# Moving one exchanged copy to ScalarE and loading four pieces together in a convolution chain with a recurrent first layer

## The chip, the cores and the metric

The kernel runs on one core of one Trainium2 chip. The metric is the device time of one execution in microseconds (us). The core has five engines with queues of their own: PE (TensorE, matmuls; its weight loads are listed as PEld), DVE (VectorE), ACT (ScalarE), POOL (GpSimd) and SP (SyncE, which here starts most of the DMA transfers). An engine works through its own instructions; between engines, order is kept by semaphores.

## The reference

Four layers follow each other on a batch of 16 images with 32 channels of 128 x 128, each with a normalisation ahead of it or a residual behind it. Two places matter here.

The first layer is a diagonal LSTM. The image is skewed, so that step t sees the diagonal column t, and 128 steps follow each other; each needs the hidden state of the step before, at its own row and at the row above:

```python
def step(carry, xt):
    pc, ph = carry
    ph_shift = jnp.pad(ph, ((0, 0), (0, 0), (1, 0)))[:, :, :-1]
    s2s = jnp.einsum('oc,bch->boh', W1_prev, ph_shift) + jnp.einsum('oc,bch->boh', W1_cur, ph) + b1[None, :, None]
    g = xt + s2s
    o = jax.nn.sigmoid(g[:, 0 * bo:1 * bo])
    f = jax.nn.sigmoid(g[:, 1 * bo:2 * bo])
    i = jax.nn.sigmoid(g[:, 2 * bo:3 * bo])
    gg = jnp.tanh(g[:, 3 * bo:4 * bo])
    nc = f * pc + i * gg
    nh = o * jnp.tanh(nc)
    return ((nc, nh), nh)
```

At step t only the rows up to t differ from each other: every later row has seen no input yet, and all such rows carry the same state. So a kernel needs to compute t + 1 rows and one more that stands for the rest.

The second layer quantises its input to 8 bits and takes sums of absolute differences with the weights:

```python
qx = _ste_quant(x, INPUT_SCALE)       # shift, clamp to +-127, round
...
return -jnp.sum(jnp.abs(pr - wk[None, :, None]), axis=1)   # for each output channel
```

The third layer (a Hartley transform) and the fourth (a small U-Net) are not touched by the change.

## The kernel before

The recurrent stage works in 16 chunks of T = 8 steps. The batch is split into two chains (c = 0, 1), each with two groups of images, so that one chain can compute while the other waits. In a chunk, n = min(8(ch + 1) + 2, 128) rows are computed. `rows(ch)` gives this n; when a new chunk begins, the rows that come in are set from the last row of the chunk before (line 210):

```python
for ch in range(NT):
    n = rows(ch)
    following = load(ch + 1) if ch + 1 < NT else None
    if ch:
        m = rows(ch - 1)
        for c in range(2):
            for v in (hs[c][(ch - 1) % 2][:, T - 1, :, 1:], ex[c][0][:, :, 1:], cs[c]):
                if n > m:
                    nc.vector.tensor_copy(v[:, :, m:n], bcast(v[:, :, m - 1], 2, n - m))   # L210
    for j in range(T):
        t = T * ch + j
        for c in range(2):
            h_in = (hs[c][ch % 2][:, j - 1] if j else hs[c][(ch - 1) % 2][:, T - 1], ex[c][t % 2])
            ...
            # 24 products into PSUM tile pg: 8 each with xn, with h and with e (L223)
            ...
            for q in (F, I, G, O):
                nc.scalar.activation(gt[:, q, :, :n], place[q][:, :, :n],          # L243
                                     AF.Tanh if q == G else AF.Sigmoid, bias=...)
            nc.vector.tensor_mul(cell, cell, gt[:, F, :, :n])                      # L250
            nc.vector.tensor_mul(ig[:, :, :n], gt[:, I, :, :n], gt[:, G, :, :n])   # L251
            nc.vector.tensor_add(cell, cell, ig[:, :, :n])                         # L252
            nc.scalar.activation(th[:, :, :n], cell, AF.Tanh)                      # L254
            nc.vector.tensor_mul(h_out[:, :, 1 : n + 1], gt[:, O, :, :n], th[:, :, :n])   # L255
            for half in range(2):
                own, other = slice(64 * half, 64 * half + 64), slice(64 - 64 * half, 128 - 64 * half)
                nc.vector.tensor_copy(ex[c][(t + 1) % 2][own, :, 1 : n + 1],
                                      h_out[other, :, 1 : n + 1])                  # L258
        # residual additions and statistics of one group: L185, L188, L189
        # normalisation of the next chunk's input on ScalarE: L174
        ...
```

`e` (the tile `ex`) is h with its two halves of 64 partitions exchanged. A product of 64 x 64 reads its operand from one half of the partitions; with h and e both halves of the PE array have work at once. A tile has 2n elements in each partition, so the shape 128x196 in the profile stands for n = 98 rows.

A scheduler decides in which order the instructions of this stage stand on each engine; within an engine the order is then fixed.

After the stage, the first image is quantised in four pieces before the second layer can begin. The pieces go through the pool `self.xp`, which has two buffers:

```python
def unquantised(self, b, i):
    t = self.xp.tile([128, 8 * W], F32, name="xq")
    self.nc.sync.dma_start(t, jc_rows(self.d["x1"], b, i // 2, 8 * (i % 2), 8))    # L482
    return t
def scaled(self, b, t):
    self.nc.scalar.activation(t, t, AF.Identity, bias=..., scale=...)              # L486
def quantise(self, b, i, t):
    qt = self.ring[i % 2]                       # two tiles in turn
    nc.vector.tensor_scalar(qt[:, :, 1 : W + 1], v, RND, RND, ALU.add, ALU.subtract)   # L493
    nc.vector.tensor_scalar(flat, flat, -127.0, 127.0, ALU.max, ALU.min)               # L495
    self.weave.later(4.0, lambda: nc.sync.dma_start(to, flat))                         # L498
...
for i in range(4):
    t = self.unquantised(0, i)
    self.scaled(0, t)
    self.quantise(0, i, t)
    weave.due(float("inf"))                     # starts the store now
before, following = None, self.loaded(0, 0)     # L505: reads the quantised image back, as tile q
```

`jc_rows` addresses a piece as 4 x 32 runs of 4 KB. Everything after this, up to the end of the kernel, is recorded in a fixed order.

Of the kernel before, what the change touches and what calls it, by code (L numbers as in the profile page):

```python
# [7 lines left out]
F32 = mybir.dt.float32  # L8
# [7 lines left out]
B, C, H, W = 16, 32, 128, 128  # L16
# [32 lines left out]
def bcast(ap, dim, n):  # L49

    dims = [list(x) for x in ap.ap]
    dims.insert(dim, [0, n])
    return bass.AP(ap.tensor, ap.offset, dims)
# [47 lines left out]
def stage0(nc, tc, keep, cst, x, xs, w0, b1, b2, x1):  # L101
# [5 lines left out]
    T = 8  # L107
# [4 lines left out]
    with ExitStack() as ctx:  # L112
# [3 lines left out]
        with tc.tile_pool(name="s0_ld", bufs=4) as ld, tc.tile_pool(name="s0_ps", bufs=2, space=PSUM) as ps:  # L116
            for g in range(NG):
                for q in range(4):
                    t = ld.tile([128, 32 * W], F32, name="x_in")
# [25 lines left out]
        hs = [[sm.tile([128, T, 2, H + 1], F32, name=f"h_{c}_{i}") for i in range(2)] for c in range(2)]  # L145
        ex = [[sm.tile([128, 2, H + 1], F32, name=f"e_{c}_{i}") for i in range(2)] for c in range(2)]
        cs = [sm.tile([128, 2, H], F32, name=f"c_{c}") for c in range(2)]
# [15 lines left out]
        def load(ch):  # L163
            steps = slice(T * ch * H, T * (ch + 1) * H)
            xn = [xp.tile([128, NG, T, H], F32, name=f"xn{i}") for i in range(2)]
            res = rp.tile([128, NG, T, H], F32, name="res")
            for g in range(NG):
                nc.sync.dma_start(flat(xn[0], g), bc_view(xs, g)[:, steps])
                nc.sync.dma_start(flat(res, g), bc_view(x, g)[:, steps])
            return xn, res  # L170

        def normalise(ch, xn, g):
            v = xn[0][:, g, :, : T * (ch + 1)]
            nc.scalar.activation(v, v, AF.Identity, bias=shift[:, g : g + 1], scale=r0[:, g : g + 1])  # L174
            for half in range(2):
                own, other = slice(64 * half, 64 * half + 64), slice(64 - 64 * half, 128 - 64 * half)
                nc.sync.dma_start(flat(xn[1], g)[own], flat(xn[0], g)[other])

        def add(ch, res, g, half):

            n = rows(ch)
            steps = slice(T // 2 * half, T // 2 * (half + 1))
            h = hs[g // 2][ch % 2][:, steps, g % 2]
            r = res[:, g, steps, :n]
            nc.vector.tensor_add(r, r, h[:, :, 1 : n + 1])  # L185
            if n < H:
                r = res[:, g, steps, n:]
                nc.vector.tensor_add(r, r, bcast(h[:, :, n], 2, H - n))  # L188
            nc.vector.bn_stats(stat1[:, g, 2 * ch + half, :], flat(res, g)[:, 512 * half : 512 * half + 512])  # L189
            if half:  # L190
                nc.sync.dma_start(bc_view(x1, g)[:, T * ch * H : T * (ch + 1) * H], flat(res, g))

        def rows(ch):

            return min(T * (ch + 1) + 2, H)
# [4 lines left out]
        with tc.tile_pool(name="s0_gps", bufs=2, space=PSUM) as gps:  # L200
            for ch in range(NT):
                n = rows(ch)
                following = load(ch + 1) if ch + 1 < NT else None
                if ch:

                    m = rows(ch - 1)
                    for c in range(2):
                        for v in (hs[c][(ch - 1) % 2][:, T - 1, :, 1:], ex[c][0][:, :, 1:], cs[c]):
                            if n > m:
                                nc.vector.tensor_copy(v[:, :, m:n], bcast(v[:, :, m - 1], 2, n - m))  # L210
                for j in range(T):
                    t = T * ch + j
                    for c in range(2):
                        h_in = (hs[c][ch % 2][:, j - 1] if j else hs[c][(ch - 1) % 2][:, T - 1], ex[c][t % 2])
                        h_out, cell = hs[c][ch % 2][:, j], cs[c][:, :, :n]
                        pg = gps.tile([128, 2, 2, 2, H], F32, name=f"pg{c}")
                        place = {q: pg[:, i, k] for i, b in enumerate(BANK) for k, q in enumerate(b)}

                        def product(kind, k, i, pair, v, width):

                            q = BANK[i][k]
                            half = slice(64 * (pair ^ i), 64 * (pair ^ i) + 64)
                            nc.tensor.matmul(  # L223
                                place[q][64 * pair : 64 * pair + 64, :, :width],
                                wb[half, 4 * kind + KIND[q]].rearrange("p b o -> p (b o)"),
                                v[half],
                                start=kind == 2 and k == 0,
                                stop=kind == 1,
                                skip_group_check=True,
                            )  # L230

                        for k in range(2):
                            for i in range(2):
                                for pair in range(2):
                                    product(2, k, i, pair, xn[i][:, 2 * c : 2 * c + 2, j, : t + 1], t + 1)
                        for k in range(2):
                            for kind in range(2):
                                for i in range(2):
                                    for pair in range(2):
                                        product(kind, k, i, pair, h_in[i][:, :, 1 - kind : n + 1 - kind], n)  # L240
                        gt = gp.tile([128, 4, 2, H], F32, name=f"gt{c}")
                        for q in (F, I, G, O):
                            nc.scalar.activation(  # L243
                                gt[:, q, :, :n],
                                place[q][:, :, :n],
                                AF.Tanh if q == G else AF.Sigmoid,
                                bias=bias[:, KIND[q] : KIND[q] + 1],
                            )
                        ig = gp.tile([128, 2, H], F32, name=f"ig{c}", bufs=1)
# [3 lines that stand above are left out]
                        th = gp.tile([128, 2, H], F32, name=f"th{c}")  # L253
                        nc.scalar.activation(th[:, :, :n], cell, AF.Tanh)  # L254
                        nc.vector.tensor_mul(h_out[:, :, 1 : n + 1], gt[:, O, :, :n], th[:, :, :n])  # L255
                        for half in range(2):
                            own, other = slice(64 * half, 64 * half + 64), slice(64 - 64 * half, 128 - 64 * half)
                            nc.vector.tensor_copy(ex[c][(t + 1) % 2][own, :, 1 : n + 1], h_out[other, :, 1 : n + 1])  # L258
                    if j >= T // 2:
                        add(ch, res, j - T // 2, 0)  # L260
                        if following:
                            normalise(ch + 1, following[0], j - T // 2)
                    elif ch:
                        add(ch - 1, previous, j, 1)
                previous = res
                if following:
                    xn, res = following
            for g in range(NG):
                add(NT - 1, previous, g, 1)
                nc.vector.bn_aggr(mv[:, g, :], stat1[:, g].rearrange("p a b -> p (a b)"))  # L270
# [16 lines left out]
def jc_rows(t, b, half, at=0, rows=16):  # L287

    first = t.offset + b * CHW + (64 * half + at) * W
    return bass.AP(t.tensor, first, [[16 * W, 4], [HW, C], [1, rows * W]])  # L290
# [123 lines left out]
class Differences:  # L414
# [61 lines left out]
                self.ring[0].rearrange("p r w -> p (r w)")[:, : 4 * P].rearrange("p (a w) -> p a w", w=P),  # L476
            )

    def unquantised(self, b, i):

        t = self.xp.tile([128, 8 * W], F32, name="xq")
        self.nc.sync.dma_start(t, jc_rows(self.d["x1"], b, i // 2, 8 * (i % 2), 8))  # L482
        return t

# [75 lines left out]
    def run(self, tc, ctx, weave):  # L560
        nc, R, P = self.nc, self.R, self.P
# [3 lines left out]
        self.qp = ctx.enter_context(tc.tile_pool(name="s1_q", bufs=2, side="right"))  # L565
        dp = ctx.enter_context(tc.tile_pool(name="s1_d", bufs=2, side="right"))
        ps = ctx.enter_context(tc.tile_pool(name="s1_ps", bufs=4, space=PSUM))
        for i in range(4):
            t = self.unquantised(0, i)
            self.scaled(0, t)  # L570
            self.quantise(0, i, t)
            weave.due(float("inf"))
        before, following = None, self.loaded(0, 0)
        for b in range(B):
            for half in range(2):
                q = following
                late, ahead, xq = [], [], {}
                for i in range(72):
# [26 lines left out]
                    t = dp.tile([128, R, P], F16, name="d_act" if act else "d_dve", bufs=2 if act else 3)  # L605
# [1211 lines left out]
```

## Time and profile before

| | |
|---|---|
| time, median of 3 runs | 7892.06 us (7889.79 to 7894.32) |
| span of the profiled execution | 7884.7 us |
| busy PE, PEld, DVE, ACT | 5635.8, 3165.4, 5847.9, 5406.7 us |
| recurrent stage | about 94 to 838 us of the span |
| first quantisation, until the second layer's first difference | about 838 to 935 us |
| mean granted clock of PE | 0.842 |

A window of the profile gives the busy time of each engine between two moments; the timeline lists instructions in order of time, those that follow each other in one group merged into one row (x4 is four instructions), with the idle time ahead of them in brackets, and after the arrow what ended it. A group of instructions is listed with its shapes and number, then its busy time and the mean of one in ns, then the idle time ahead of it. Waits are put down to whatever came last.

### The profile page before, as it was taken

Reading aid. Unit: us, or ns where it says so; the run is one execution under the profiler, and the core shown is the slowest. Engines: PE = TensorE matmul, PEld = TensorE weight load, DVE = VectorE, ACT = ScalarE, POOL = GpSimd, SP = SyncE. Lnnn points to the kernel's source line nnn. Section 1 sums busy time; section 2 is a strip of 40 time slices with the busy share of each in tenths; the row PEclk is TensorE's granted clock in tenths of the full one; section 3 lists DMA queues with packets and bytes.
Section 4 is the critical chain, followed back from the end, with each engine's and each line's share of the span. In section 5 each row is a group of like instructions: output and inputs, shape, how many; then the busy total and the mean of one; then the engine's idle time right before and its main releaser. Section 6 shows DMA issues by size and latency. Waiting matters only on the chain. (4 is left out here: it accounts for less than half of the span.)

```text
span 7884.7 us, 258419 instructions
## 1 busy us (share of the span) xinstructions
PE 5635.8 (71%) x121132; PEld 3165.4 (40%) x121132; DVE 5847.9 (74%) x7177; ACT 5406.7 (69%) x3129; POOL 21.6 (0%) x15
## 2 busy tenths in 40 slices
PE   3788366566677668886676666897667765997797
PEld 3665222222253334442343343343335333555564
DVE  7787599989969797887877978888787877134213
ACT  2565488799869879887778877887887885123122
POOL 0000000000000000000000000000000000000000
PEclk9899788888878779998868788998787887897896
DMA  8653111111132431112332432120333233434314
GB/s 319 223 181 130 59 50 60 48 52 39 50 116 80 123 102 51 58 33 67 79 98 90 129 89 73 40 70 34 88 86 101 87 102 94 116 107 122 91 33 90
DMA packets 374269, 721.68 MB, mean 92 GB/s; under 512 B 50896, under 2 KB 219856, under 8 KB 362320
## 3 DMA queue, kind: packets, MB, share of 16 engines
q1 hardware_dynamic: 372768, 704.58, 29.4%
q8 instruction: 949, 15.55, 0.8%
q14 instruction: 120, 0.98, 0.0%
q10 hardware_dynamic: 432, 0.57, 0.0%
HBM read 507.21 MB, written 164.32 MB: 85 GB/s over the span
## 5 line engine op out<-in xcount | busy, mean ns | idle before, releaser
L610 ACT ACTIVATE d_act<-q,neg 128x8192 f16<-128x8192 f16 (+1 forms) x612 | 4332.5, 7137 | 930.9 <-PE acc L536 877.6
L614 DVE TENSOR_SCALAR d_dve<-q,qw 128x8192 f16<-128x8192 f16 (+1 forms) x1692 | 3906.2, 2361 | 512.0 <-PE acc L536 476.3
L536 PE MATMUL acc<-d_dve,sel 128*32 128x512 f16 x27072 | 2007.5, 432 | 861.6 <-DVE d_dve L614 838.8
L536 PEld LDWEIGHTS <-sel 128*32 128x32 f16 x36864 | 1121.1, 106 | 2800.6 <-issue 2196.8
L536 PE MATMUL acc<-d_act,sel 128*32 128x512 f16 x9792 | 784.5, 446 | 499.1 <-ACT d_act L610 494.7
L1519 PE MATMUL acc<-xp,wf 32*32 32x512 f32 x25600 | 986.0, 625 | 29.0 <-issue 16.1
L1519 PEld LDWEIGHTS acc<-xp,wf 32*32 32x32 f32 x25600 | 478.8, 105 | 378.1 <-issue 244.6
L1458 ACT ACTIVATE y<-pooled,b 32x128 f32<-32x128 f32 x512 | 204.6, 400 | 532.2 <-DVE pooled L1444 525.1
L223 PE MATMUL pg<-h,wb 64*64 64x20 f32 (+15 forms) x4096 | 401.2, 323 | 102.4 <-DVE h L255 67.0
L753 PE MATMUL acc<-y,u_conv 32*32 32x256 f32 (+1 forms) x9728 | 402.2, 511 | 79.3 <-issue 35.8
L223 PE MATMUL pg<-e,wb 64*64 64x20 f32 (+15 forms) x4096 | 353.2, 318 | 24.7 <-DVE e L258 10.0
L243 ACT ACTIVATE gt<-pg,bias 128x20 f32<-128x20 f32 (+15 forms) x1024 | 302.7, 377 | 84.2 <-PE pg L223 80.0
L1204 PE MATMUL acc<-xp 32*64 32x204 f32 (+3 forms) x8576 | 247.3, 368 | 130.0 <-ACT xp L1170 107.8
L552 PE MATMUL acc<-q,sel 32*32 32x512 f16 x4608 | 158.6, 556 | 204.9 <-DVE xr L519 115.1
L223 PEld LDWEIGHTS pg<-h,wb 64*64 64x64 f32 x4096 | 243.7, 156 | 140.5 <-DVE h L255 97.6
L223 PEld LDWEIGHTS pg<-e,wb 64*64 64x64 f32 x4096 | 250.6, 158 | 108.3 <-DVE e L258 77.9
L223 PE MATMUL pg<-xn,wb 64*64 64x8 f32 (+60 forms) x4096 | 267.9, 304 | 25.3 <-ACT gt L243 17.4
L1616 ACT ACTIVATE xr<-xr,l_ms 128x1024 f32<-128x1024 f32 x64 | 70.4, 1141 | 305.6 <-DVE xr L1611 254.3
L753 PEld LDWEIGHTS acc<-y,u_conv 32*32 32x32 f32 x9728 | 189.7, 119 | 220.0 <-issue 126.5
L1164 ACT ACTIVATE xp<-xp,fr_shift,stats 128x1280 f32<-128x1280 f32 (+1 forms) x128 | 181.7, 1431 | 136.1 <-DMA xp<-x_d 73.9
L1204 PEld LDWEIGHTS acc<-xp 32*64 32x64 f32 (+1 forms) x8576 | 199.3, 147 | 187.8 <-ACT xp L1170 118.0
L254 ACT ACTIVATE th<-c 128x20 f32<-128x20 f32 (+15 forms) x256 | 81.9, 320 | 222.2 <-DVE c L252 221.2
(203 smaller groups left out, 4247.9 us busy)
## 6 DMA issues: line engine op xcount, KB each, us to landing
xr<-x_d SPq DMA_DIRECT2D x192, 512.0 KB
xp<-x_d SPq DMA_DIRECT2D x112, 640.0 KB
q<-q_d SPq DMA_DIRECT2D x32, 2145.0 KB
x_d<-xr SPq DMA_DIRECT2D x128, 512.0 KB
x_in<-in_x_dram SPq DMA_DIRECT2D x16, 2048.0 KB
res<-in_x_dram SPq DMA_DIRECT2D x64, 512.0 KB
xn<-in_xs_dram SPq DMA_DIRECT2D x64, 512.0 KB
xn<-xn SPq DMA_DIRECT2D x128, 256.0 KB
```

Source lines behind the costliest of these rows:

```text
L223: nc.tensor.matmul(place[q][64 * pair : 64 * pair + 64, :, :width], wb[half, 4 * kind + KIND[q]].rearrange("p b o -> p (b o)"), v[half], s ...
L243: nc.scalar.activation(gt[:, q, :, :n], place[q][:, :, :n], AF.Tanh if q == G else AF.Sigmoid, bias=bias[:, KIND[q] : KIND[q] + 1],)
L254: nc.scalar.activation(th[:, :, :n], cell, AF.Tanh)
L536: self.nc.tensor.matmul(acc[k][32 * j : 32 * j + 32, :], self.sel16[:, i // 9, :], d[:, row : row + 4, c : c + W], start=False, stop=i == 71,)
L552: self.nc.tensor.matmul(acc[k][32 * j : 32 * j + 32, :], self.sel16[rows, 8, :], q[rows, row : row + 4, kw : kw + W], start=tap == 0, stop ...
L610: nc.scalar.activation(dst, src, AF.Relu, bias=self.neg[:, i : i + 1])
L614: nc.vector.tensor_scalar(dst, src, self.qw[:, i : i + 1], 0.0, ALU.subtract, ALU.max)
L753: nc.tensor.matmul(acc[blk][32 * j : 32 * j + 32, o : o + rows * n], t[part, 4 * par + tap, :], src[part, top : top + rows, left : left + ...
L1164: nc.scalar.activation(v, v, AF.Identity, bias=shift[0], scale=self.stats3[:, 1])
L1204: nc.tensor.matmul(gram[blk][j : j + width, at : at + n], xp[part, l, 2 + j : 2 + j + width], xp[part, rows, j : j + width + 4], start=sta ...
L1458: nc.scalar.activation(d, s, AF.Identity, bias=bj)
L1519: nc.tensor.matmul(acc[blk][32 * j : 32 * j + 32, :], tap_of("all", tap)[rows], xp[rows, 4 * j + kh : 4 * j + kh + 4, kw : kw + W], start= ...
```

## The change

Three things are changed, none of which alters the values that are computed.

The rows that come into the next chunk are set behind their own chain's last step (j = T - 1), not at the head of the next chunk; this is meant to let one chain go on without the other's last step. One of the two copies from h to e goes to ScalarE, so that the two halves can be copied side by side and VectorE has less to do. And the first image's four pieces are loaded together into a pool of four buffers of its own, so that the loads need not follow each other.

```diff
             for ch in range(NT):
                 n = rows(ch)
                 following = load(ch + 1) if ch + 1 < NT else None
-                if ch:
-
-                    m = rows(ch - 1)
-                    for c in range(2):
-                        for v in (hs[c][(ch - 1) % 2][:, T - 1, :, 1:], ex[c][0][:, :, 1:], cs[c]):
-                            if n > m:
-                                nc.vector.tensor_copy(v[:, :, m:n], bcast(v[:, :, m - 1], 2, n - m))
                 for j in range(T):
...
                         nc.vector.tensor_mul(h_out[:, :, 1 : n + 1], gt[:, O, :, :n], th[:, :, :n])
-                        for half in range(2):
-                            own, other = slice(64 * half, 64 * half + 64), slice(64 - 64 * half, 128 - 64 * half)
-                            nc.vector.tensor_copy(ex[c][(t + 1) % 2][own, :, 1 : n + 1], h_out[other, :, 1 : n + 1])
+                        e_out = ex[c][(t + 1) % 2]
+                        nc.scalar.copy(e_out[:64, :, 1 : n + 1], h_out[64:, :, 1 : n + 1])
+                        nc.vector.tensor_copy(e_out[64:, :, 1 : n + 1], h_out[:64, :, 1 : n + 1])
+                        if j == T - 1 and n < H:
+
+                            m = rows(ch + 1)
+                            for v in (h_out[:, :, 1:], e_out[:, :, 1:], cs[c]):
+                                nc.vector.tensor_copy(v[:, :, n:m], bcast(v[:, :, n - 1], 2, m - n))
...
-    def unquantised(self, b, i):
-
-        t = self.xp.tile([128, 8 * W], F32, name="xq")
+    def unquantised(self, b, i, pool=None):
+
+        t = (pool or self.xp).tile([128, 8 * W], F32, name="xq")
...
-        for i in range(4):
-            t = self.unquantised(0, i)
-            self.scaled(0, t)
-            self.quantise(0, i, t)
-            weave.due(float("inf"))
+        with tc.tile_pool(name="s1_x0", bufs=4, side="right") as pool:
+            xq = [self.unquantised(0, i, pool) for i in range(4)]
+            for i in range(4):
+                self.scaled(0, xq[i])
+                self.quantise(0, i, xq[i])
+                weave.due(float("inf"))
```

In the changed kernel the ScalarE copy stands in line 250, the VectorE copy in line 251, and the copies for the incoming rows in line 256.

## The prediction

> **What bounds the kernel now.** I read the windows first, to see how much of the span the two changed places hold. Columns: window, its length, busy us (and instructions) of PE, weight loads, DVE, ACT, POOL, then granted clock, DMA share, GB/s.
>
> ```profile
> 94.00:838.00 744.00, 585.26 (x12288) 444.19 (x12288) 574.12 (x2003) 424.99 (x1346) 0.00 (x0) 0.94 0.55 177
> 838.00:935.00 97.00, 2.69 (x32) 2.35 (x48) 14.82 (x48) 5.80 (x7) 2.21 (x3) 0.50 0.23 72
> ```
>
> The recurrent stage is 744 us of 7885, the first quantisation 97; the other 6950 us from 935 on keep their instructions in the changed build, so they only shift. In the recurrent stage no engine is full: PE 79%, DVE 77%, ACT 57%. That reads like VectorE with ScalarE to spare, and invites moving work over. But with two chains alternating, what counts is the loop through the engines. So I went to the timeline, at 98 rows (196 elements a partition), one step of one chain and the start of the next (start, length, engine, line, names, shape; in brackets the idle time before it and what ended it):
>
> ```profile
> 570.49 0.37 ACT L254 ACTIVATE th<-c 128x196 f32<-128x196 f32 x1 [0.57 <-DVE c L252]
> ...
> 570.88 0.36 DVE L255 TENSOR_TENSOR h<-gt,th 128x196 f32<-128x196 f32 x1 [0.49 <-ACT th L254]
> 570.97 1.37 ACT L243 ACTIVATE gt<-pg,bias 128x196 f32<-128x196 f32 x4
> ...
> 571.35 0.53 DVE L258 COPY e<-h 64x196 f32<-64x196 f32 x2
> 571.91 0.36 DVE L250 TENSOR_TENSOR c<-c,gt 128x196 f32<-128x196 f32 x1
> 571.93 0.14 PEld L223 LDWEIGHTS pg<-e,wb 64*64 64x64 f32 x2 [0.44 <-DVE e L258]
> ...
> 573.04 0.37 ACT L254 ACTIVATE th<-c 128x196 f32<-128x196 f32 x1 [0.70 <-DVE c L252]
> ...
> 573.44 0.37 DVE L255 TENSOR_TENSOR h<-gt,th 128x196 f32<-128x196 f32 x1 [0.49 <-ACT th L254]
> 573.59 1.37 ACT L243 ACTIVATE gt<-pg,bias 128x196 f32<-128x196 f32 x4 [0.18 <-PE pg L223]
> ```
>
> Three things are to be seen. Chain A's th ends at 570.86, and ScalarE starts the four gates of chain B 0.11 us later, at 570.97: it does not wait for A's h, which ends at 571.24. Then the gates (1.37), 0.70 idle while VectorE makes the cell, th (0.37), 0.18 idle for PE: one chain-step takes 2.55 us, so ScalarE is committed for all but those gaps. And PE waits 0.44 us for the exchanged copy e, which is what the change aims at.
>
> **What the Trainium skill says.** Three places. "PSUM — Partial Sum Buffer", section "Engine vs sequencer instructions": the queues of ScalarE and VectorE are strict FIFO. The trace agrees as far as it shows: gates and tanh run in the order in which they stand, and 0.70 us of ScalarE stay empty ahead of a tanh. "VectorE: DVE Perf Modes", section "The TRN2 errata": a ScalarE copy within SBUF takes 224 cycles plus one per element at 1.2 GHz, so 293 ns at 128 elements. The group of such copies elsewhere in this kernel measures 297:
>
> ```profile
> L1168 ACT COPY xp<-xp 128x128 f32<-128x128 f32 x16 | 4.8, 297 | 0.4
> L258 DVE COPY e<-h 64x20 f32<-64x20 f32 (+15 forms) x510 | 116.6, 229 | 25.7 <-DVE h L255 0.5 <-issue 0.2
> ```
>
> At 196 elements that gives an estimate of 0.35 us, against 0.26 for a VectorE copy of that size (0.53 for two, above). "DMA: Bandwidth & Descriptors", section "Why a DMA increments its semaphore by 16 and not by 1": a transfer uses as many DMA engines as divide its slowest dimension. The sample's pieces have an outer dimension of 4, hence four of 16; in the trace the packets of these transfers overlap fourfold at most, and the DMA share of the second window is only 0.23.
>
> **Part 1, the incoming rows.** 15 chunk boundaries with six copies (L210, about 0.17 us each, 15.5 us in all on VectorE) stay; only their place in the source moves. PE sits idle 32.5 us for the h copies of L210 (22 times, from the list of waits), which looks like the prize. But in the built order of before, the scheduler had already put each chain's row copies directly behind that chain's last step: cell rows after the cell, h rows after the two e copies, e rows next. The built order of after is the same but for one e copy fewer. The long PE waits there come from the additions and statistics (L185, L188, L189) that stand on VectorE at the same places. I give this part 0 us.
>
> **Part 2, one copy to ScalarE.** It removes 256 VectorE copies (half of the 116.6 us in the group above, 58 us) and adds 256 ScalarE copies. Where it stands decides. In the built order of after, from 66 rows on, ScalarE's row is gates, th, copy, gates, th, copy, with hardly an exception; at 58 rows mostly so. The copy needs h, and h needs th. So ScalarE, having finished A's th, waits for A's h, copies, and only then begins B's gates, which PE had ready. Between th's end and the next gates at 196 elements: h ends 0.38 to 0.40 after th; 0.10 from VectorE's end to ScalarE's start (cell to th in the timeline); copy 0.35; about 0.08 back because instructions that follow each other overlap. That makes 0.77 in place of 0.11 to 0.18: **about 0.6 us more per chain-step**, 3.15 in place of 2.55. At 256 elements: 0.46 + 0.10 + 0.41 - 0.08 = 0.89 against a median gap of 0.29, so 0.6 again; at 116 elements 0.62 against a gap of about zero. e itself comes hardly sooner: 0.03 + 0.36 + 0.10 + 0.35 after th, where two VectorE copies gave 0.03 + 0.36 + 0.11 + 0.53. That 0.2 us is no gain, since PE will no longer be what ends last: its result for B is ready about 1 us before ScalarE asks.
>
> How many steps count: each chunk has 16 chain-steps. Four are lengthened by two additions with statistics each on VectorE (at 98 rows 12 steps take 2.56 and the chunk 49.6 us, so these four take about 4.7). In them ScalarE is idle anyway, and VectorE starts the additions one copy (0.26 us) earlier: 64 such steps, perhaps 0.2 each, -13 us. The other 12: ten chunks from 58 to 128 rows, 10 x 12 x 0.6 = +72 us. In the six early chunks the order is mixed and VectorE the fuller engine; the same sum there gives 0 to 0.4 per step, about 13 us, of which VectorE's relief may return half: +6. Stage: 72 + 6 - 13 = **+65 us**.
>
> **Part 3, four buffers loaded together.** The timeline of the second window:
>
> ```profile
> 855.30 0.56 SPq L482 DMA_DIRECT2D xq<-x_d  x1
> ...
> 867.35 1.24 ACT L486 ACTIVATE xq<-xq,shift,r 128x1024 f32<-128x1024 f32 x1 [13.95 <-DMA xq<-x_d]
> 868.62 0.69 DVE L493 TENSOR_SCALAR qt<-xq 128x1024 f16<-128x1024 f32 x1 [11.98 <-ACT xq L486]
> ...
> 900.10 0.52 SPq L498 DMA_DIRECT2D q_d<-qt  x1
> 900.78 0.53 SPq L505 DMA_DIRECT2D q<-q_d  x1
> ...
> 934.73 6.91 DVE L614 TENSOR_SCALAR d_dve<-q,qw 128x8192 f16<-128x8192 f16 x3 [34.67 <-DMA q<-q_d]
> ```
>
> Load, scale, round, store, and only then the next load: a round of 15.1 us, three times between 854.7 and 900.1. After, three loads go out near 847 to 850. Were they free, the last store would leave near 871 and 29 us were saved. But loads and stores share four DMA engines: packets of a load run for about 6 us, those of a store about 5. From 849.5, three loads (18) and four stores (20) end near 887.5; before, the last store's packets end near 907. So **-19 us**, between -15 and -28. It lies on the path: PE and VectorE wait for q until 934.7.
>
> **Sum.** 7892 + 65 - 19 = 7938; I say 7936.
>
> **The rivals.** First, that VectorE is the bound and its relief wins. For it: DVE busy 80 to 90% in chunks; PE's waits for e (77.9 us in weight loads) and the additions that delay the cell. Then up to 58 us come off, minus some ScalarE waiting; with part 3 near 7830 to 7870. Against it: in the undisturbed steps VectorE idles 0.49 ahead of each h, and ScalarE's order is rigid. Second, that the row copies were the barrier: PE idle 39 us in weight loads at L210, 15 boundaries x 2 us = -30 us, with part 3 alone some 7845; against it the unchanged order. Third, that ScalarE's wait is longer than I count: the four normalisations per chunk (L174, 1.08 us) stand between the gates, too, and may no longer fit in its gaps; 15 chunks x 2 us more, 7965.
>
> **Range and chances.** The term of +72 could be 40 (if gates start sooner, or fewer steps count) or 95; the loads -15 to -28; the third rival adds up to 30. That gives 7900 to 7972. A gain of 2% is 158 us, more than the whole of VectorE's relief; a loss of 2% would need over 0.8 us on every one of 256 steps plus no gain from the loads. Chances: faster 0.01, same 0.96, slower 0.03.
>
> **What would show it.** Right: idle time of ScalarE ahead of the new copy, ended by h, some 0.4 us each and about 100 us in sum; PE's wait for e nearly gone but waits of PE for h and of VectorE for gates grown; chain-steps of 3.1 to 3.2 us at 98 rows; the stage near 810 us; the window from its end to the first difference near 78. Wrong: if steps at 98 rows stay at 2.6 or fall, if the copy stands behind the other chain's gates, or if the boundary steps shrink by 2 us.

## The result, and the profile after

The changed kernel takes 7920.26 us (median of 4 runs, 7912.21 to 7931.19), the kernel before 7890.93 us on the same chip (7886.52 to 7894.32). The ratio is 1.0038, with a 95% interval from 1.0021 to 1.0056: slower, by some 29 us, and within the 2%.

The windows of the changed kernel, cut at the same two events as before (end of the recurrent stage, first difference of the second layer), show where it went. Columns as before: window, length, busy us (and instructions) of PE, weight loads, DVE, ACT, POOL, granted clock, DMA share, GB/s.

```profile
94.00:885.00 791.00, 583.61 (x12288) 469.05 (x12288) 526.99 (x1748) 508.62 (x1601) 0.00 (x0) 0.93 0.52 167
885.00:966.00 81.00, 2.88 (x44) 2.38 (x49) 14.47 (x48) 7.23 (x8) 2.22 (x3) 0.50 0.29 88
```

The recurrent stage is 791 us long in place of 744, the first quantisation 81 in place of 97. VectorE gave up 47 us (574 to 527) and ScalarE took 84 (425 to 509). Neither is full, and the stage is longer all the same. The timeline of two chain-steps at 90 rows says why:

```profile
569.30 0.35 ACT L247 ACTIVATE th<-c 128x180 f32<-128x180 f32 x1 [0.55 <-DVE c L245]
...
569.68 0.35 DVE L248 TENSOR_TENSOR h<-gt,th 128x180 f32<-128x180 f32 x1 [0.48 <-ACT th L247]
570.06 0.34 ACT L250 COPY e<-h 64x180 f32<-64x180 f32 x1 [0.41 <-DVE h L248]
...
570.13 0.25 DVE L251 COPY e<-h 64x180 f32<-64x180 f32 x1
570.43 1.32 ACT L236 ACTIVATE gt<-pg,bias 128x180 f32<-128x180 f32 x4
...
570.87 0.35 DVE L243 TENSOR_TENSOR c<-c,gt 128x180 f32<-128x180 f32 x1 [0.49 <-ACT gt L236]
...
572.30 0.35 ACT L247 ACTIVATE th<-c 128x180 f32<-128x180 f32 x1 [0.55 <-DVE c L245]
```

ScalarE ends its tanh at 569.65 and then does nothing until 570.06, although the other chain's gates (the row at 570.43) wait for nothing but ScalarE: the copy stands ahead of them and needs h. From th to the next th a chain-step takes 3.00 us; in the kernel before it took 2.45 to 2.46 at 90 rows. VectorE, which had the cell to compute right behind its copies before, is now idle for 0.49 us in front of the cell, because the gates come late.

The list of ScalarE's waits in the stage, first of before (us in total, times, longest):

```profile
ACT th L254 <- DVE c L252: 220.9, 222, 4.8
ACT gt L243 <- PE pg L223: 76.1, 124, 3.3
ACT xn L174 <- DMA xn<-in_xs_dram: 9.1, 11, 1.9
```

and of the changed kernel:

```profile
ACT th L247 <- DVE c L245: 155.8, 202, 3.8
ACT e L250 <- DVE h L248: 79.8, 196, 0.8
ACT gt L236 <- PE pg L216: 33.4, 42, 4.5
```

A wait of 79.8 us, 196 times 0.41, is new, and the normalisations' wait for DMA (9.1) is gone. ScalarE got 79.8 us of waiting and 83.6 us of work more; the waits for the cell and for PE shrank by 107.8, with the 9.1 by 116.9. The balance, 79.8 + 83.6 - 116.9 = 46.5 us, is the growth of the window (47) but for small gaps. The weight loads of PE in the changed kernel and, behind them, the same two groups of before show the aim of the copy reached, to no use:

```profile
L216 PEld LDWEIGHTS pg<-e,wb 64*64 64x64 f32 x4096 | 268.7, 157 | 49.0 <-DVE e L251 18.8
...
L216 PEld LDWEIGHTS pg<-h,wb 64*64 64x64 f32 x4096 | 242.7, 155 | 222.3 <-DVE h L248 179.6
```

```profile
L223 PEld LDWEIGHTS pg<-h,wb 64*64 64x64 f32 x4096 | 243.7, 156 | 140.5 <-DVE h L255 97.6
L223 PEld LDWEIGHTS pg<-e,wb 64*64 64x64 f32 x4096 | 250.6, 158 | 108.3 <-DVE e L258 77.9
```

Idle time put down to e fell from 77.9 to 18.8 us, that put down to h rose from 97.6 to 179.6.

### The profile page after: what moved, and what is told of

Same layout as the page of the kernel before. It is cut to its first block, busy times and chain, and to the rows that moved or that the text cites. A ratio compares the mean times of both kernels' runs of the same rounds, so it can differ in the third digit from the quotient of the medians.

```text
span 7922.1 us, 258265 instructions
## 1 busy us (share of the span) xinstructions
PE 5667.7 (72%) x121132; PEld 3212.0 (41%) x121132; DVE 5798.7 (73%) x6921; ACT 5492.0 (69%) x3385; POOL 21.9 (0%) x15
## 5 line engine op out<-in xcount | busy, mean ns | idle before, releaser
L216 PE MATMUL pg<-h,wb 64*64 64x20 f32 (+15 forms) x4096 | 374.4, 321 | 162.9 <-DVE h L248 126.5
L216 PEld LDWEIGHTS pg<-h,wb 64*64 64x64 f32 x4096 | 242.7, 155 | 222.3 <-DVE h L248 179.6
L216 PEld LDWEIGHTS pg<-e,wb 64*64 64x64 f32 x4096 | 268.7, 157 | 49.0 <-DVE e L251 18.8
L550 PE MATMUL acc<-q,sel 32*32 32x512 f16 x4608 | 161.9, 568 | 165.2 <-DVE xr L517 114.2
L1639 DVE TENSOR_SCALAR s<-acc,l_ms,l_one 128x512 f32<-128x512 f32 x128 | 100.7, 809 | 172.7 <-PE acc L752 172.7
```

Of the source, the lines that this page charges most:

```text
L216: nc.tensor.matmul(place[q][64 * pair : 64 * pair + 64, :, :width], wb[half, 4 * kind + KIND[q]].rearrange("p b o -> p (b o)"), v[half], s ...
L550: self.nc.tensor.matmul(acc[k][32 * j : 32 * j + 32, :], self.sel16[rows, 8, :], q[rows, row : row + 4, kw : kw + W], start=tap == 0, stop ...
L1639: nc.vector.tensor_scalar(s.rearrange("p b r w -> p (b r w)"), acc[blk], istd[:, blk : blk + 1], one[:, blk : blk + 1], ALU.mult, ALU.add,)
```

## The experiments

All stage lengths below are read from the timelines, from the end of the first h to the end of the last h. "To q" is the time from the last h to the first packet of the read of q, "q read" from there to the first difference.

| kernel | time, us | against before, same chip | stage | to q | q read |
|---|---|---|---|---|---|
| before | 7890.93 | | 732.6 | 68.0 | 29.2 |
| changed | 7920.26 | +29.3 | 777.9 | 41.6 | 39.1 |
| ScalarE copy alone | 7938.16 | +34.8 | 777.7 | 66.9 | 28.9 |
| four loads alone | 7876.81 | -26.6 | 733.5 | 42.6 | 34.5 |
| rows alone | 7898.44 | -4.9 | 736.5 | 67.2 | 29.0 |
| rows and loads | 7879.15 | -24.2 | 736.8 | 42.7 | 34.2 |
| the same, and ScalarE work without a wait | 7888.47 | -13.8 | 743.4 | 41.7 | 31.3 |
| changed, copy on GpSimd | 7851.61 | -50.6 | 709.3 | 41.4 | 37.4 |
| changed, copy behind the gates | 8016.4 (one run) | +114.2 | 833.8 | 41.8 | 35.3 |
| rows and loads, on 16 DMA engines | 7848.63 | -53.6 | 736.8 | 30.8 | 12.2 |
| copy on GpSimd and 16 DMA engines | 7804.11 | -77.6 | 712.7 | 29.6 | 12.7 |

The experiments ran on several chips, so times are to be compared through the third column. The time after the first difference, in which no instruction is changed, lies between 6932.5 and 6998.3 us in these profiles. That scatter belongs to single executions, so the stage lengths, read from one execution each, are sharper than differences of whole times. Kernels with the same instructions in the recurrent stage agree within 1 us in two cases (732.6 and 733.5; 736.5, 736.8 and 736.8), and differ by 3.4 in a third (709.3 and 712.7). The first four experiments separate the parts, the next three the cause inside the copy, the last two spread the transfers over more DMA engines, without and with the copy on GpSimd.

### The ScalarE copy alone

The kernel before, with only this edit:

```diff
-                        for half in range(2):
-                            own, other = ...
-                            nc.vector.tensor_copy(ex[c][(t + 1) % 2][own, :, 1 : n + 1], h_out[other, :, 1 : n + 1])
+                        e_out = ex[c][(t + 1) % 2]
+                        nc.scalar.copy(e_out[:64, :, 1 : n + 1], h_out[64:, :, 1 : n + 1])
+                        nc.vector.tensor_copy(e_out[64:, :, 1 : n + 1], h_out[:64, :, 1 : n + 1])
```

> The kernel before with one change, the copy of one half of h to ScalarE. My theory (ScalarE's queue waits for h between tanh and the other chain's gates) expects about 47 us over before, near 7938: in the changed kernel the stage grew from 837.6 to 884.9 us at its end. The rival that the row copies or the loads caused part of the stage's growth expects less than 35 us.

Measured: 7938.16 us against 7903.36 for before on the same chip, ratio 1.0048 (1.0035 to 1.0061). The stage is 777.7 us, the changed kernel's to within 0.2. The whole lengthening of the stage is this copy's. By whole times the copy costs 34.8 us (28 to 48 by the interval), just under the 35 that was the rival's mark; the stage, 45.1 us longer than before, decides against the rival.

### The four loads alone

```diff
-        for i in range(4):
-            t = self.unquantised(0, i)
+        with tc.tile_pool(name="s1_x0", bufs=4, side="right") as pool:
+            xq = [self.unquantised(0, i, pool) for i in range(4)]
+            for i in range(4):
```

> The kernel before with one change, the four pieces loaded together. Expected 17 us under before, near 7874: the way from the last step to the first packet of q shrinks by 26 us, but in the changed kernel q's own transfer took about 9 us longer. If that longer transfer was chance, 26 us; then q's packets take 641 ns at the median again.

Measured: 7876.81 against 7903.36, ratio 0.9968 (0.9956 to 0.9981). The stage stays (733.5). The read of q starts 25.4 us sooner after the stage, but lasts 5.3 us longer until the first difference, together 20.1 us less. The whole times give 26.6 (15 to 35 by the interval), the figure that was expected if the longer read of q were chance; but the packets of q take 984 ns at the median here, not 641, so it is not.

### The rows alone

```diff
+                        if j == T - 1 and n < H:
+                            m = rows(ch + 1)
+                            for v in (h_out[:, :, 1:], e_out[:, :, 1:], cs[c]):
+                                nc.vector.tensor_copy(v[:, :, n:m], bcast(v[:, :, n - 1], 2, m - n))
```

The copies at the chunk's head are taken out, as in the change; both copies to e stay on VectorE.

> The kernel before with one change, the incoming rows set behind their chain's last step. My theory expects no difference (within 4 us), since the scheduler had put these copies there already. The rival that they were a barrier between the chains expects 20 to 30 us less.

Measured: 7898.44 against 7903.36, ratio 0.9991 (0.9981 to 1.0001), stage 736.5 against 732.6. No gain: the row copies were no barrier. Whether the 4 us more of stage are real is open, as they are about what one stage code differs by between two profiles.

### Rows and loads, without the ScalarE copy

The changed kernel with one call put back:

```diff
-                        nc.scalar.copy(e_out[:64, :, 1 : n + 1], h_out[64:, :, 1 : n + 1])
+                        nc.vector.tensor_copy(e_out[:64, :, 1 : n + 1], h_out[64:, :, 1 : n + 1])
```

> The changed kernel with both copies of h on VectorE again. If the three parts add up: 17 to 26 us under before, 46 to 50 under the changed kernel, near 7870.

Measured: 7879.15 against 7903.36, ratio 0.997 (0.9962 to 0.9978), stage 736.8. Against this kernel the ScalarE copy costs the changed one 777.9 - 736.8 = 41.1 us of stage; from the first h to the first difference the two are 44.9 us apart, just under the 46 to 50 expected. This kernel is the base for what follows.

### ScalarE's work without its wait

Is it the copy's 0.35 us on ScalarE that costs, or the wait for h ahead of it? Here both copies to e are on VectorE, and ScalarE does a copy of the same size in the same place between tanh and gates; but it copies th, which ScalarE has itself just made, into a tile that nobody reads. It is work added, nothing is left out.

```diff
                         nc.scalar.activation(th[:, :, :n], cell, AF.Tanh)
+                        spare = gp.tile([128, 2, H], F32, name=f"sp{c}")
+                        nc.scalar.copy(spare[:64, :, :n], th[64:, :, :n])
```

> Both copies of h to e on VectorE (as in e4), and ScalarE makes a copy of the same size at the same place in its queue, behind the tanh and ahead of the other chain's gates, but of the tanh itself into a spare tile that nothing reads. So ScalarE does the work and does not wait for VectorE's h. My theory that the wait costs, not the copy, expects steps of about 2.7 us at 98 rows and a recurrent stage 10 to 25 us longer than the 736.8 of e4. The rival that ScalarE simply has too much to do expects the 778 of the changed kernel.

Measured: 7888.47 against 7902.22, ratio 0.9981 (0.9971 to 0.999), stage 743.4, 6.6 above the base. ScalarE's and VectorE's rows of the timeline at 98 rows:

```profile
600.17 0.37 ACT L247 ACTIVATE th<-c 128x196 f32<-128x196 f32 x1 [0.51 <-DVE c L245]
600.57 0.35 ACT L249 COPY sp<-th 64x196 f32<-64x196 f32 x1
600.95 1.37 ACT L236 ACTIVATE gt<-pg,bias 128x196 f32<-128x196 f32 x4
602.84 0.37 ACT L247 ACTIVATE th<-c 128x196 f32<-128x196 f32 x1 [0.51 <-DVE c L245]
```

```profile
597.91 0.36 DVE L250 TENSOR_TENSOR h<-gt,th 128x196 f32<-128x196 f32 x1 [0.43 <-ACT th L247]
598.38 0.26 DVE L252 COPY e<-h 64x196 f32<-64x196 f32 x1
598.65 0.26 DVE L253 COPY e<-h 64x196 f32<-64x196 f32 x1
598.94 0.36 DVE L243 TENSOR_TENSOR c<-c,gt 128x196 f32<-128x196 f32 x1
```

The gates start 0.41 us after the tanh ends, where they started 0.11 to 0.18 after it before. Yet a chain-step takes 2.67 us (600.17 to 602.84), against 2.55 before. The second list shows why the work is nearly free: the cell starts right behind the two e copies, 1.43 us after the start of its tanh at 597.51; before it was 1.42 (570.49 to 571.91). While VectorE copies, ScalarE has time for its copy. So in this kernel the work costs about 0.1 us a step, where a copy of the same size that needs h costs 0.56 (2.56 to 3.12 at 98 rows). ScalarE is as busy as in the changed kernel, so the rival that it simply has too much to do falls.

### The copy on GpSimd

The changed kernel, with the copy on an engine that has nothing else to do in the stage:

```diff
-                        nc.scalar.copy(e_out[:64, :, 1 : n + 1], h_out[64:, :, 1 : n + 1])
+                        nc.gpsimd.tensor_copy(e_out[:64, :, 1 : n + 1], h_out[64:, :, 1 : n + 1])
```

> As the changed kernel, but the copy that went to ScalarE is made by GpSimd, which has nothing else to do in this stage. If ScalarE's queue is the cause, the stage is back near 737 us or below, as long as a GpSimd copy of 196 elements takes no more than about 0.4 us; each 0.1 us above that lengthens a chain's loop, about 0.05 us per chain-step or some 10 us in all. The rival that splitting the two copies over two engines is itself harmful expects 778.

Measured: 7851.61 against 7902.22, ratio 0.9935 (0.9919 to 0.995). The stage is 709.3 us, 27.5 below the base and 68.6 below the changed kernel, in which VectorE also makes one of the two copies. The timeline at 98 rows:

```profile
561.32 0.37 ACT L247 ACTIVATE th<-c 128x196 f32<-128x196 f32 x1 [0.57 <-DVE c L245]
...
561.69 1.37 ACT L236 ACTIVATE gt<-pg,bias 128x196 f32<-128x196 f32 x4
561.72 0.36 DVE L248 TENSOR_TENSOR h<-gt,th 128x196 f32<-128x196 f32 x1 [0.49 <-ACT th L247]
...
562.19 0.26 DVE L251 COPY e<-h 64x196 f32<-64x196 f32 x1
562.24 0.41 POOL L250 COPY e<-h 64x196 f32<-64x196 f32 x1 [2.24 <-DVE h L248]
```

GpSimd waits for h, 2.24 us, and nobody stands behind it; ScalarE goes from tanh to gates without a gap. The two copies run side by side, and VectorE's takes 0.26 us as it did alone. The Trainium skill, "Perfetto Trace Analysis", section "Optimizing Scalar/DVE Operations", says that work of a full VectorE may go to ScalarE or even to GpSimd, and that GpSimd may not help because the two share a port to SBUF. Here it is the other way about: off to ScalarE +41.1 us of stage, off to GpSimd -27.5, and VectorE's copy beside it is not slowed (at 196 elements 256 ns at the median, 257 in the base).

### The copy behind the other chain's gates

If the wait ahead of the gates is the fault, why not set the copy behind them? The edit puts off the copy until the other chain's four gates are recorded, with an ordering edge to the last of them; the incoming row of e follows the copy.

```diff
+                        def owed(...):
+                            nc.scalar.copy(e_out[:64, :, 1 : n + 1], h_out[64:, :, 1 : n + 1])
+                            if len(pending) > 1:
+                                behind(pending[1])          # ordered after the last gate
+                        pending = [owed]                    # called after the next step's gates
```

> As the changed kernel, but each ScalarE copy is forced behind the other chain's four gates. Then ScalarE never waits for h, and e comes late: gates of B 1.37, copy about 0.3, products with e 1.9, then the gates of A, so about 3.6 us per chain-step at 98 rows, a stage 130 to 170 us longer than before's 733. If the order in ScalarE's queue did not matter, it would stay near 778.

Measured: 8016.4 us in one run, against 7902.22, so without an interval; the stage is 833.8 us, 97 above the base. In the timeline at 98 rows:

```profile
618.95 1.37 ACT L246 ACTIVATE gt<-pg,bias 128x196 f32<-128x196 f32 x4 [1.01 <-PE pg L226]
...
620.34 0.35 ACT L271 COPY e<-h 64x196 f32<-64x196 f32 x1
...
620.74 0.13 PEld L226 LDWEIGHTS pg<-e,wb 64*64 64x64 f32 x1 [1.48 <-ACT e L271]
...
620.89 0.37 ACT L261 ACTIVATE th<-c 128x196 f32<-128x196 f32 x1 [0.20 <-DVE c L259]
```

The copy waits for nothing now, but it ends at 620.69, and the h that it copies was ready at 618.33: 2.36 us, where VectorE's copy of the same h was done after 0.37. PE's weight loads wait 1.48 us for e, and the gates 1.01 us for PE. A step takes 3.44 us. Between tanh and gates the copy delays the gates; behind them it delays the products that the gates after them need. Neither of the two places tried on ScalarE is good; a place between two of the four gates was not tried.

### The first sample's transfers on 16 DMA engines

The base, with the first sample's four loads, four stores and the first read of q each cut into four transfers of 32 partitions, so that 32 channels, not four runs, are the slowest dimension:

```diff
-        self.nc.sync.dma_start(t, jc_rows(self.d["x1"], b, i // 2, 8 * (i % 2), 8))
+            for j in range(4):
+                part = bass.AP(src.tensor, src.offset + 16 * j * W, [list(v) for v in src.ap[1:]])
+                self.nc.sync.dma_start(t[32 * j : 32 * j + 32], part)
...
+                self.nc.sync.dma_start(
+                    q[32 * j : 32 * j + 32], bass.AP(q_d.tensor, first, [[(H + 2) * P, C], [1, (self.R + 2) * P]])
+                )
```

> As e4, with each transfer of the first sample (the four loads, the four stores, the first read of q) cut into four of 32 partitions, so that its slowest dimension is 32 in place of 4. If four DMA engines are what bounds this stretch, the way from the last step to the first difference falls from 77 us by about 35 to 45 (a read of q in about 8 us, no more lining up of stores behind loads), and the kernel ends near 7840. The rival that latency and SyncE's issue time (0.55 us each) bound it expects less than 15 us.

Measured: 7848.63 against 7902.22, ratio 0.9928 (0.9916 to 0.994). The window of the first quantisation in the kernel with the four loads alone, and then in this one:

```profile
839.00:916.00 77.00, 2.44 (x16) 2.14 (x16) 14.62 (x49) 6.29 (x6) 2.22 (x3) 0.50 0.28 89
```

```profile
842.00:885.00 43.00, 4.21 (x19) 2.43 (x20) 14.93 (x49) 6.20 (x6) 2.22 (x3) 0.50 0.65 159
```

43 us in place of 77, at a DMA share of 0.65 in place of 0.28. By the Trainium skill, "DMA: Bandwidth & Descriptors", section "Why a DMA increments its semaphore by 16 and not by 1", the slowest dimension decides how many of the 16 DMA engines a transfer uses, and the run agrees: of the packets of q's first read at most four overlap in the base, and sixteen here. So with four buffers the transfers no longer waited for buffers, but for four engines. The read of q takes 12.2 us in place of 34.2, so 22 of the 34 us gained are the read's, which used four engines in the kernel before as well. The gain of 34 us is just under the 35 to 45 expected and far above the 15 of the rival, latency and issue time.

### Both

```diff
-                        nc.scalar.copy(e_out[:64, :, 1 : n + 1], h_out[64:, :, 1 : n + 1])
+                        nc.gpsimd.tensor_copy(e_out[:64, :, 1 : n + 1], h_out[64:, :, 1 : n + 1])
```

with the transfers of the experiment before.

> e6 and e8 together: the copy on GpSimd, and the first sample's transfers cut for 16 DMA engines. They touch different stretches, so the sum is expected: a stage of 709 us (e6) and 43 us from the last step to the first difference (e8), together some 61 us under before, near 7840 where before measures 7902. If the two share something, for one the DMA engines' access to the same buffers, it is less.

Measured: 7804.11 against 7881.67, ratio 0.9904 (0.9887 to 0.992). It beats the kernel before by 77.6 us, and with it the changed kernel. Stage and first quantisation add up: 712.7 and 29.6 + 12.7 are within 4 us of what each edit gave by itself. The 61 us that were expected were a wrong sum: its own parts, 733 to 709 and 97 to 43, make 78.

## Why the prediction was right, and which terms were off

The prediction (7936 in 7900 to 7972) held: the mechanism is the one it gave, and the time is 15.7 us lower. It had the change 44 us slower (7892 to 7936), and it is 29.3 slower.

**Part 1 was right.** 0 us was said. The rows alone are 0.9991 (0.9981 to 1.0001), and nothing got shorter by 2 us a boundary. PE's weight loads wait 39.1 us for the h row copies before, 38.5 with the rows alone and 40.8 in the changed kernel. The rival of the row copies as the barrier falls.

**Part 2: right mechanism, with sizes off that add up to 20 us.** The sum was 72 - 13 + 6 = +65; the stage grew by 45.3. The two timelines can be cut by chunk and kind of step. A step is here the time from the end of one h to the end of the next; the long ones are the 1st, 8th, 9th and 16th of a chunk's 16.

| term of the prediction | said | found |
|---|---|---|
| the other 12 steps of the ten chunks from 58 rows | +72 | +60.5 (307.0 to 367.5) |
| the four long steps of these ten chunks | -8 of the -13 | -9.7 (194.4 to 184.7) |
| the six early chunks, all steps | +6, and -5 of the -13 | -5.4 (231.2 to 225.8) |

The step at 98 rows was to go from 2.55 to 3.15 us and went from 2.56 to 3.12; at 128 rows it went from 2.95 to 3.55. In the changed kernel:

```profile
616.82 0.37 ACT L247 ACTIVATE th<-c 128x196 f32<-128x196 f32 x1 [0.57 <-DVE c L245]
617.22 0.36 DVE L248 TENSOR_TENSOR h<-gt,th 128x196 f32<-128x196 f32 x1 [0.49 <-ACT th L247]
617.62 0.35 ACT L250 COPY e<-h 64x196 f32<-64x196 f32 x1 [0.43 <-DVE h L248]
...
618.00 1.37 ACT L236 ACTIVATE gt<-pg,bias 128x196 f32<-128x196 f32 x4
...
619.94 0.37 ACT L247 ACTIVATE th<-c 128x196 f32<-128x196 f32 x1 [0.57 <-DVE c L245]
```

The gates start 0.81 us after the tanh ends, where 0.77 was said. Within that, two readings were off and nearly cancel: the copy starts 0.03 us after h, not 0.10, and the gates start 0.03 us after the copy ends, not 0.08 before it. The copy itself, estimated at 0.35 us, takes 0.353. What was left out is that ScalarE's idle time ahead of the tanh also shrinks, from 0.64 to 0.57 us. So a typical step grew by 0.56 us, but the twelve on average by 0.50 (60.5 / 120): before, some of them were already longer than the rest (two at 58 rows took 3.18 and 3.12 us, where 2.07 was typical), and these grew little or shrank. The early chunks failed: the prediction let ScalarE's delay outweigh VectorE's relief there by about 1 us, and relief won by 5. The long steps gained 0.24 us each (9.7 / 40), close to the 0.2 said and to the one copy of 0.26 us by which the additions move up.

What inside the copy costs is narrowed down by the two experiments on it. Work in the same slot that needs no other engine costs 6.6 us of stage. VectorE's relief brings 27.5 when the copy goes where no one waits behind it. The changed kernel has both and stands at +41.1 over the base, so if the terms add, the wait for h is 41.1 + 27.5 - 6.6 = 62 us. That they add is not shown, and is doubtful: the work was measured with both copies on VectorE, which give ScalarE time for it. With only one copy there, ScalarE's work may cost more, and part of the 62 us would be the work's. The GpSimd kernel with that extra work on ScalarE would tell, and was not run.

**Part 3: right in sum, by two errors that partly cancel.** -19 was said, and 97.2 us from the last h to the first difference became 80.7, which is -16.5. But the transfers ahead of the read of q came out 26.4 us shorter, near the upper end of 15 to 28, and the read itself 9.9 us longer, which the prediction did not have. The first error is the length of the stores. The prediction let the three loads' packets end 29.9 us after the last h and the four stores need 20 us more. The loads' packets end at 914.08, 29.1 us after the last h (884.93), but the stores' end at 927.72, only 13.6 us later: a store whose packets took 6.0 us alone before takes less when several stand in line. Something of the old waiting is left. In the changed kernel's timeline

```profile
917.49 0.70 DVE L491 TENSOR_SCALAR qt<-xq 128x1024 f16<-128x1024 f32 x1 [9.63 <-DMA q_d<-qt]
...
920.30 0.70 DVE L491 TENSOR_SCALAR qt<-xq 128x1024 f16<-128x1024 f32 x1 [1.50 <-DMA q_d<-qt]
...
924.93 0.54 SPq L503 DMA_DIRECT2D q<-q_d  x1
...
965.60 11.47 DVE L613 TENSOR_SCALAR d_dve<-q,qw 128x8192 f16<-128x8192 f16 x5 [43.11 <-DMA q<-q_d]
```

the third and fourth piece wait for the first two stores (9.63 and 1.50 us), as two tiles serve all four, and the read of q is issued 3.9 us after the last piece is rounded (921.00 to 924.93), behind the fourth store in the queue; for 2.8 us of them SyncE waits until a store has landed. The second error: the packets of q's first read, 17,160 bytes each, take 648 ns at the median in the three kernels without the four loads (before, ScalarE copy alone, rows alone), and between 788 and 1165 ns in the six kernels that have the four loads on four engines (changed, and the four-loads, rows-and-loads, work-without-wait, GpSimd and behind-the-gates kernels); many are at 1270 to 1330, about twice 641, and others lie between. So it comes with the four loads, and it takes back part of what they bring: the read lasts 31.3 to 39.1 us in these six kernels, 28.9 to 29.2 in the three. Why is open: four engines that fetch the same rows in step is one guess, and it was not tried.

**The signs that were named** came: ScalarE idle 0.41 us ahead of each copy, 79.8 us in all where about 100 was said; PE's waits for e mostly gone and those for h grown; VectorE's waits for the gates ahead of the cell up from 25.6 to 88.0 us; the stage's window 791 where 810 was said; the second window 81 where 78 was said.

**The rivals.** VectorE's relief as the winner falls for this kernel, but its premise was sound: it is worth 27.5 us, of up to 58 us moved, when GpSimd takes the copy. At 98 rows the undisturbed step only goes from 2.56 to 2.50 there, because the loop of gates, cell and tanh remains; of the 27.5 us, some 12 come from the twelve shorter steps of the ten later chunks, 6 from their long steps and 10 from the early chunks. The third rival, that the normalisations would no longer fit, shows no sign: the stage is shorter than was said, and ScalarE still has 155.8 us of waiting for the cell. One sum in the chances was wrong: a loss of 2% is 158 us, which over 256 steps is 0.62 us a step, not 0.8.

Two sizes were off in the experiments, too. Work without the wait cost less than was expected of it, because VectorE's two copies left ScalarE the time for it. The copy behind the gates cost less as well: 3.44 us a step, and a stage 101 us longer than before.

The parts measured alone (+34.8, -26.6, -4.9 us from the medians) sum to +3 us, the changed kernel to +29. Each has an interval of some 10 us on either side, and by the lengths from the first h to the first difference the same parts sum to +27.4 (+43.7, -19.2, +2.9) and the changed kernel is +28.8 longer. So no interaction is needed, but the medians of whole times alone would not have shown that.

## What to carry to other kernels

Before an operation is moved to an engine with idle time, look at what its input waits for: in an in-order queue the operation brings that wait with it, and everything that stands behind waits too. Here 0.35 us of work without such a wait cost about 0.1 us a step, and the same with it 0.56; the engine that won is one with nothing urgent behind the operation, though it is slower at it. And when loads are made independent by more buffers, count the DMA engines they use: the next limit was four engines of sixteen, and spreading the transfers, with the buffers in place, brought 34 us, 22 of them in the read behind the loads, where the buffers had brought 20.

## What was not expected of the hardware

- GpSimd's copy of 64 partitions of fp32 takes 197 ns (all medians) at 20 elements, 413 at 196 and 494 at 256; ScalarE's 207, 353 and 404; VectorE's 171, 257 and 290. At these sizes GpSimd is within a quarter of ScalarE.
- The tanh on ScalarE starts 0.09 us after the end of VectorE's cell at the median, but only 0.03 us in the kernel with the work without a wait, and the ScalarE copy starts 0.03 us after the end of h. Why they differ is open. VectorE's h starts 0.03 us after the end of ScalarE's tanh.
- The packets of 17,160 bytes, four reads of the same source rows, take from 639 to 1522 ns on four engines, many of them about 641 or about twice that, as told above; on sixteen engines 1335 to 1344 ns at the median.
